# Values of the attention stream done for two steps at once, with small work in odd steps

## The chip, the cores and the metric

The kernel runs on one core of a Trainium2 chip. The core has a matrix engine (PE, TensorE), a vector engine (DVE), a scalar engine (ACT), GpSimd (POOL) and a queue engine (SP), which run side by side and meet at semaphores; 128 partitions of on-chip memory (SBUF); and PSUM, eight banks of 128 x 512 fp32[...]. The metric is the device time of one launch in microseconds; a run's result is the median of its repetitions.

## The reference

One transformer layer on x of shape (2, 2048, 256), all fp32: attention, a layer norm, then a feed-forward part with eight experts, and a last layer norm.

```python
qkv = x @ qkv_w + qkv_b                        # 16 heads of 16
q, k = rot(q), rot(k)                          # angle by head, not by position
scores = einsum('bhqd,bhkd->bhqk', q, k) / 4
out = einsum('bhqk,bhkd->bhqd', softmax(scores), v)
x = layernorm(x + out @ out_w + out_b)
n = layer_norm(x, g1, be1)
x1 = x + n + (n @ mix_w + mix_b)
n = layer_norm(x1, g2, be2)                    # 4096 tokens
topw, topi = top_k(softmax(n @ router_w), 2)   # 2 of 8 experts
y = silu(n @ w1[e] + b1[e]) @ w2[e] + b2[e]    # 256 -> 1024 -> 256
x = layernorm(x + x1 + sum over the two experts of topw * y)
```

Attention is the larger part: for each of 2 x 16 heads, 2048 x 2048 scores.

## The kernel before, in words

**Tiling of the attention.** A visit is one batch entry, one block of 512 queries and one group of four heads: 2 x 4 x 4 = 32 visits. A visit has 16 steps, one for each tile of 128 keys, so the stream has 512 steps (`NSTEP`). Queries and keys lie in two pair tiles (`qm`, `km`), two heads each, in 64 partitions per head: 16 head dimensions four times over, as high and low parts of the fp32 values[...].

**A step.** `scores` runs for both pairs: for each of four heads one matmul of keys by queries and one that subtracts the row's maximum, both on 64 rows of the array, two heads side by side. ACT takes the exponential of each 128 x 512 tile into SBUF (`ex`, L484-485, eight buffers). `values` multiplies the exponentials of a step by the values: four heads, each on 32 columns of the array at once; PE records eight matmuls for a call, two waves of four. The products of a visit's 16 steps add up in one PSUM bank (`av`), with a row of ones giving the softmax's sum. After the last step `attn_out` copies the bank to SBUF (`avs`), and `divide` turns it and divides by the sum.

**The maxima ahead.** The row maxima for a visit are computed 20 steps ahead (`AHEAD`) by `maxima`: each half step does two matmuls of 128 queries by 512 keys into two banks, and DVE reduces each bank to one column (`pm`, L434). A step has two halves, `max_step(t + AHEAD, 0)` and `max_step(t + AHEAD, 1)`. When a visit's maxima are done, `maxima_done` puts them in form on DVE and `rows_of` transposes them two steps later.

**Banks.** Four banks hold scores (`ps_sc`), one `av`, and three serve in rotation as `ps_mx`: the maxima take two per half, and every small item of PE takes its bank from the same three (`bank`).

**Small work.** All else in the stream is cut into items. `later(steps, fn, cost, urgent)` puts an item in one of two heaps by its due step; `work(budget)` takes due items until their costs use up the budget. Items of cost 2.0 are the projections to q and k (`prep_qk`), to v (`prep_v`), and the two products of a block's chain (`project`, `mix`, by way of `two_products`: eight matmuls, then on DVE an add, L568, and batch statistics, L571-572). `logits`, `bias` and `add_bias` cost 1.0, groups of four transposes 0.5 (`turned`, `prep_x`, `rows_of`, `divide`), the choice of experts 0.1 and 0.3 (`second`, `places`); loads and what runs on ACT, DVE or POOL alone cost nothing. The chain of a block of 512 tokens starts when its four visits are done, and is spread over the next 64 steps; that of the last block runs between the matmuls of the experts.

**The order.** The loop over t writes the order of PE, ACT, DVE and SP by hand (`manual_schedule`): scores of step t, first half of the maxima, small work, values of step t - 1, second half of the maxima. Each engine executes in that order; POOL is scheduled by the framework.

**Around it.** Ahead of the loop the weights are rotated (`wqk`, from `wr` and the table `cs`, with scratch tiles `t1`, `t2`), the first keys and queries are prepared, and the first 20 steps of maxima run. After it the tokens, sorted by expert into lists in DRAM, go through 46 tiles of experts (`load_tile`, `hidden`, `add_tile`), and the last layer norm.

Of the kernel before, what the change touches and what calls it, by code (L numbers as in the profile page):

```python
# [24 lines left out]
F32 = mybir.dt.float32  # L25
# [3 lines left out]
ALU = mybir.AluOpType  # L29
# [3 lines left out]
P = 128  # L33
B, S, D = 2, 2048, 256
H, HD = 16, 16
# [28 lines left out]
def seq_postln_kernel(  # L64
# [85 lines left out]
    bp = ctx.enter_context(tc.tile_pool(name="chain", bufs=1))  # L150
    ps_mx = ctx.enter_context(tc.tile_pool(name="ps_mx", bufs=3, space=PSUM))

    with ExitStack() as actx:

        ep = actx.enter_context(tc.tile_pool(name="early", bufs=1))
        ap_ = actx.enter_context(tc.tile_pool(name="attn", bufs=1))
# [4 lines left out]
        wqk = ep.tile([P, 2, 2, H, HD], F32, name="wqk")  # L161
# [23 lines left out]
        def load_x(b, tb):  # L185
            n = b * TPB + tb

            pool, tag, bufs = (ap_, f"km{tb % 2}", 3) if b == 0 else (ep, "x_in", 1)
            x_in[b, tb] = pool.tile([P, 4, D], F32, name=f"x_in_{n}", tag=tag, bufs=bufs)
            nc.sync.dma_start(out=x_in[b, tb], in_=xv[n])  # L190

        with tc.tile_pool(name="wraw", bufs=1) as wp:
            wr = bp.tile([P, 2, H, 3, HD], F32, name="wr", tag="zx", bufs=1)
            cs = wp.tile([P, 2, H, 8], F32, name="cs")
            load_x(0, 0)
            nc.scalar.dma_start(
                out=wr.rearrange("p c h t d -> p c (h t d)"),
# [59 lines left out]
            for c in range(2):  # L257
                for s in range(2):
                    u1, u2 = wr[:, c, :, s, 0:8], wr[:, c, :, s, 8:16]
                    for dst, a, b_, op in (  # L260
                        (wqk[:, c, s, :, 0:8], u1, u2, ALU.subtract),
                        (wqk[:, c, s, :, 8:16], u2, u1, ALU.add),
                    ):
                        t1 = wp.tile([P, H, 8], F32, name="t1", tag="t1", bufs=2)
                        t2 = wp.tile([P, H, 8], F32, name="t2", tag="t2", bufs=2)
                        nc.vector.tensor_mul(t1, a, cs[:, 0])
                        nc.vector.tensor_mul(t2, b_, cs[:, 1])
                        nc.vector.tensor_tensor(dst, t1, t2, op)
                nc.vector.tensor_copy(wv[:, c], wr[:, c, :, 2, :])
# [16 lines left out]
        now = [0]  # L286
# [6 lines left out]
            heappush(todo[0 if urgent else 1], (now[0] + steps, count[0], cost, fn))  # L293

        def work(budget):
            for heap in todo:
                while heap and heap[0][0] <= now[0] and budget > 0:
                    _, _, cost, fn = heappop(heap)
                    fn()
                    budget -= cost  # L300

        held: set = set()

# [10 lines left out]
        def bank(name, *shape):  # L314

            if leading[0]:
                return ps_sc.tile([P, *shape], F32, name=name, tag="sc")
            return ps_mx.tile([P, *shape], F32, name=name, tag="mx")
# [147 lines left out]
        def scores(w, kt, pair):  # L466
            sc = [ps_sc.tile([P, 512], F32, name="ps_sc", tag="sc") for _ in range(2)]
            for j in range(2):
                r = slice(64 * j, 64 * j + 64)
                nc.tensor.matmul(  # L470
                    sc[j],
                    lhsT=km[w][pair][r, kt * P : (kt + 1) * P],
                    rhs=qm[w][pair][r, :],
                    start=True,
                    stop=False,
                )
            for j in range(2):
                r = slice(64 * j, 64 * j + 64)
                nc.tensor.matmul(  # L479
                    sc[j], lhsT=sel[pair][r, :], rhs=mrow[w][r, :], start=False, stop=True  # L480
                )
            out = []
            for j in range(2):
                ex = ap_.tile([P, 512], F32, name="ex", tag="ex", bufs=8)  # L484
                nc.scalar.activation(ex, sc[j], AF.Exp, scale=0.25)  # L485
                out.append(ex)
            return out
# [4 lines left out]
        def values(w, kt, exs):  # L492
            b, _, g = visits[w]
            if kt == 0:
                av_of[w] = ps_av.tile([P, 512], F32, name=f"av_{w}", tag="av")
            av = av_of[w]
            for h in range(4):

                at = 17 * (4 * g + h)
                nc.tensor.matmul(  # L500
                    av[32 * h : 32 * h + 32, :],
                    lhsT=vt[b][:, kt, at : at + 32],
                    rhs=exs[h],
                    start=(kt == 0),
                    stop=(kt == 15),
                )
            if kt == 15:
                attn_out(w)

        def attn_out(w):  # L510

            b, qb, g = visits[w]
            av = av_of.pop(w)
            avs = bp.tile([P, 512], F32, name="avs", tag="avs", bufs=2)
            nc.scalar.copy(avs, av)
            if g == 0:
                otok[b, qb] = bp.tile([P, 4, D], F32, name=f"otok_{b}_{qb}", tag="otok", bufs=1)

            def divide():
                ps = bank("ps_o", 4, P)  # L520
                for i in range(4):
                    nc.tensor.transpose(ps[:, i, :], avs[:, i * P : (i + 1) * P], ident)  # L522
                psv = ps.rearrange("p i (h c) -> p i h c", c=32)
                rd = bp.tile([P, 4, 4], F32, name="rd", tag="rd", bufs=2)
                nc.vector.reciprocal(rd, psv[:, :, :, HD])
                nc.vector.tensor_tensor(
                    otok[b, qb][:, :, g * 64 : (g + 1) * 64].rearrange(
                        "p i (h d) -> p i h d", d=HD
                    ),
                    psv[:, :, :, 0:HD],  # L530
                    rd.unsqueeze(3).to_broadcast([P, 4, 4, HD]),
                    ALU.mult,
                )
                if g == G - 2:
                    residual(b, qb)
                if g == G - 1:
                    later(1, lambda: holding("chain", block, b, qb))

            later(1, divide, 0.5, urgent=True)
# [524 lines left out]
        with tc.manual_schedule(engines={ET.PE, ET.Activation, ET.DVE, ET.SP}):  # L1064
            for t in range(AHEAD):
                now[0] = t - AHEAD
                for half in range(2):
                    max_step(t, half)
                work(1.0)
            leading[0] = False  # L1070
            before = None
            for t in range(NSTEP):
                now[0] = t
                w, kt = divmod(t, 16)
                exs = scores(w, kt, 0) + scores(w, kt, 1)
                max_step(t + AHEAD, 0)
                work(1.0)
                if before is not None:
                    values(*before)
                max_step(t + AHEAD, 1)  # L1080
                before = (w, kt, exs)
            values(*before)
            now[0] = NSTEP

    wtp = ctx.enter_context(tc.tile_pool(name="weights", bufs=1))
# [111 lines left out]
    with tc.manual_schedule(engines={ET.PE, ET.Activation, ET.DVE, ET.SP}):  # L1197
# [3 lines left out]
        before = None  # L1201
        for t in range(NTILE):
# [8 lines left out]
            before = (t, xg, w2t, hT)  # L1211
# [119 lines left out]
```

## Time and profile before

| | us |
|---|---|
| median of 3 runs | 2401.39 (2400.65 to 2401.86) |
| the profiled execution | 2406.82 |
| its span, first to last instruction | 2405.1 |
| of it ahead of the stream's first score | 123.7 |
| the stream, 512 steps | 123.7 to 1793.3 |
| experts and last norm | 1793.3 to 2405.1 |
| busy PE / DVE / ACT / POOL | 2277.9 / 1534.9 / 1374.4 / 512.7 |
| busy in the stream (1669.6) PE / DVE / ACT | 1634.1 / 1351.4 / 1168.2 |

The times that follow come from one profiled execution. PEld is the loading of the stationary operand, which overlaps PE. A line of groups gives line, engine, operation, output<-inputs, shapes and count, then busy time and mean ns of one, then the idle time of the engine ahead of them with what ended it. The chain that ended last is followed back from the last instruction, at each step to what released it. PE's records are starts as measured and ends as modelled, so the text reckons with starts. The mean granted clock of TensorE is 0.972; it is 1.00 from about 200 to 1800 us.

### The profile page before, as it was taken

Reading aid. Unit: us, or ns where it says so; the run is one execution under the profiler, and the core shown is the slowest. Engines: PE = TensorE matmul, PEld = TensorE weight load, DVE = VectorE, ACT = ScalarE, POOL = GpSimd, SP = SyncE. Lnnn points to the kernel's source line nnn. Section 1 sums busy time; section 2 is a strip of 40 time slices with the busy share of each in tenths; the row PEclk is TensorE's granted clock in tenths of the full one; section 3 lists DMA queues with packets and bytes.
Section 4 is the critical chain, followed back from the end, with each engine's and each line's share of the span. In section 5 each row is a group of like instructions: output and inputs, shape, how many; then the busy total and the mean of one; then the engine's idle time right before and its main releaser. Section 6 shows DMA issues by size and latency. Waiting matters only on the chain.

```text
span 2405.1 us, 39739 instructions
## 1 busy us (share of the span) xinstructions
PE 2277.9 (95%) x14270; PEld 1363.8 (57%) x14270; DVE 1534.9 (64%) x3060; ACT 1374.4 (57%) x2722; POOL 512.7 (21%) x863
## 2 busy tenths in 40 slices
PE   5899999999999999999999999999998899999993
PEld 2444555545545555555555555555547788888883
DVE  2678778868877887888888888888825111111113
ACT  1167667757766776777777667777773222223333
POOL 6212221140123022011211202202122322222113
PEclk7799999999999999999999999999999899999997
DMA  7516541141124211111311211221045466567994
GB/s 217 153 42 182 144 115 54 54 132 53 53 72 123 87 55 58 58 45 54 115 45 54 71 45 53 89 71 53 1 138 168 142 193 180 176 182 225 291 292 151
DMA packets 175516, 269.69 MB, mean 112 GB/s; under 512 B 29776, under 2 KB 109656, under 8 KB 175320
## 3 DMA queue, kind: packets, MB, share of 16 engines
q1 hardware_dynamic: 142648, 213.26, 25.9%
q0 software_dynamic: 32256, 52.98, 10.1%
q8 instruction: 113, 1.85, 0.3%
q10 hardware_dynamic: 416, 0.92, 0.1%
q14 instruction: 83, 0.68, 0.1%
HBM read 204.29 MB, written 62.74 MB: 111 GB/s over the span
## 4 chain that ended last, share of the span: by engine, by line
PE 77%; DVE 16%; DMA 3%; ACT 2%; issue 1%; POOL 1%; another core or an unknown queue 0%; SPq 0%; ACTq 0%; DVEq 0%; POOLq 0%
PE av L500 19%; PE ps_mx L426 13%; DVE pm L434 12%; PE ps_h L1161 11%; PE ps_y L1176 10%; PE ps_sc L470 6%; PE ps_sc L479 6%; PE ps_qk L345 2%; DMA st<-full 2%; PE ps_v L371 1%; PE ps_p L561 1%; PE ps_mix L561 1%; PE ps_m L458 1%; PE ps_o L522 1%; PE ps_b L766 1%
## 5 line engine op out<-in xcount | busy, mean ns | idle before, releaser
L434 DVE TENSOR_REDUCE pm<-ps_mx 128x1 f32<-128x512 f32 x2048 | 1273.2, 682 | 218.3 <-PE ps_mx L426 209.3
L485 ACT ACTIVATE ex<-ps_sc 128x512 f32<-128x512 f32 x2048 | 1058.1, 603 | 453.7 <-PE ps_sc L479 433.7
L426 PE MATMUL ps_mx<-km,qm 64*128 64x512 f32 x2048 | 580.5, 474 | 36.4 <-DMA km<-st 15.3
L426 PEld LDWEIGHTS ps_mx<-km,qm 64*128 64x128 f32 x2048 | 297.7, 186 | 556.2 <-DVE pm L434 357.4
L500 PE MATMUL av<-ex,vt 128*32 128x512 f32 x4096 | 547.3, 606 | 0.0
L470 PE MATMUL ps_sc<-qm,km 64*128 64x512 f32 x2048 | 435.4, 396 | 0.4 <-ACT ex L485 0.3
L479 PE MATMUL ps_sc<-mrow,sel 64*128 64x512 f32 x2048 | 428.6, 392 | 0.0
L1168 ACT ACTIVATE hT<-ps_h,b 128x256 f32<-128x256 f32 (+1 forms) x368 | 156.3, 425 | 378.3 <-PE ps_h L1161 361.9
L1161 PE MATMUL ps_h<-xT,w 128*128 128x256 f32 (+1 forms) x1472 | 282.6, 342 | 17.2 <-issue 11.0
L1161 PEld LDWEIGHTS ps_h<-xT,w 128*128 128x128 f32 x1472 | 231.6, 193 | 62.4 <-ACT hT L1168 21.7
L1176 PE MATMUL ps_y<-w,hT 128*128 128x256 f32 x1136 | 253.7, 379 | 0.0
L479 PEld LDWEIGHTS ps_sc<-mrow,sel 64*128 64x128 f32 x2048 | 216.7, 185 | 40.5
L470 PEld LDWEIGHTS ps_sc<-qm,km 64*128 64x128 f32 x2048 | 214.8, 186 | 42.0 <-ACT ex L485 18.3
L1176 PEld LDWEIGHTS ps_y<-w,hT 128*128 128x128 f32 x1136 | 212.1, 190 | 27.5 <-issue 0.7
L1140 DVE TENSOR_SCALAR xT<-ps_x,cols_sb 128x256 f32<-128x256 f32 (+1 forms) x92 | 40.2, 478 | 271.4 <-PE ps_x L1136 271.4
L1187 POOL DMA_INDIRECT acc<-y,xg x71 | 110.1, 1551 | 390.8 <-DVE y L1186 307.0
L500 PEld LDWEIGHTS av<-ex,vt 128*32 128x32 f32 x4096 | 80.9, 108 | 133.7 <-issue 132.6
L1186 DVE TENSOR_SCALAR y<-ps_y,xg 128x256 f32<-128x256 f32 x71 | 34.2, 483 | 187.8 <-PE ps_y L1176 187.6
L132 POOL TENSOR_SCALAR op_mul<-mv 128x4 f32<-128x4 f32 x18 | 4.2, 233 | 492.7 <-DVE mv L572 491.7
L358 POOL TENSOR_TENSOR full<-full,hi 128x512 f32<-128x512 f32 x32 | 40.9, 1279 | 239.5 <-DVE hi L354 239.4
L345 PE MATMUL ps_qk<-xT,wqk 128*128 128x512 f32 x128 | 73.3, 700 | 4.8 <-ACT xT L336 1.5
L857 POOL DMA_INDIRECT x_list<-zx,at_i x64 | 64.1, 1002 | 16.5 <-issue 13.6
(198 smaller groups left out, 1160.4 us busy)
## 6 DMA issues: line engine op xcount, KB each, us to landing
w<-in_w SPq DMA_DIRECT2D x92, 1024.0 KB
km<-st SPq DMA_DIRECT2D x256, 256.0 KB
st<-hi POOLq DMA_DIRECT2D x64, 256.0 KB
st<-full POOLq DMA_DIRECT2D x64, 256.0 KB
qm<-st SPq DMA_DIRECT2D x64, 256.0 KB
xg<-x_list SPq DMA_DIRECT2D x25, 258.0 KB
x_in<-in_x SPq DMA_DIRECT2D x8, 512.0 KB
xr<-in_x SPq DMA_DIRECT2D x8, 512.0 KB
```

Of the source, the lines that this page charges most:

```text
L345: nc.tensor.matmul(ps, lhsT=wqk[:, c, s, 8 * hh : 8 * hh + 8, :].rearrange("p h d -> p (h d)"), rhs=xT[b, tb][:, c, :], start=(c == 0), st ...
L426: nc.tensor.matmul(ps[j], lhsT=qm[w][pair][r, qt * P : (qt + 1) * P], rhs=km[w][pair][r, kb * 512 : (kb + 1) * 512], start=True, stop=True,)
L434: nc.vector.tensor_reduce(pm[w][:, qt, 2 * pair + j, kb : kb + 1], ps[j], AX.X, ALU.max)
L470: nc.tensor.matmul(sc[j], lhsT=km[w][pair][r, kt * P : (kt + 1) * P], rhs=qm[w][pair][r, :], start=True, stop=False,)
L479: nc.tensor.matmul(sc[j], lhsT=sel[pair][r, :], rhs=mrow[w][r, :], start=False, stop=True)
L485: nc.scalar.activation(ex, sc[j], AF.Exp, scale=0.25)
L500: nc.tensor.matmul(av[32 * h : 32 * h + 32, :], lhsT=vt[b][:, kt, at : at + 32], rhs=exs[h], start=(kt == 0), stop=(kt == 15),)
L857: ins = nc.gpsimd.indirect_dma_start(out=x_list, out_offset=bass.IndirectOffsetOnAxis(ap=at_i[:, k, i : i + 1], axis=0), in_=zx[:, k, i, : ...
L1161: nc.tensor.matmul(ps, lhsT=w1t[:, c, k * P : (k + 1) * P], rhs=xT[:, c, :], start=(c == 0), stop=(c == 1),)
L1168: nc.scalar.activation(hT[:, k, :], ps, AF.Silu, bias=b1[:, k : k + 1])
L1176: nc.tensor.matmul(ps, lhsT=hT[:, k, s * P : (s + 1) * P], rhs=w2t[:, k, :], start=(k == 0), stop=(k == NFC - 1),)
L1187: nc.gpsimd.indirect_dma_start(out=acc, out_offset=bass.IndirectOffsetOnAxis(ap=xg[:, s, D : D + 1].bitcast(I32), axis=0), in_=y, in_offse ...
```

## The change

In an odd step due small work is done with the budget 1.0. If its costs come to 0.4 or more, no values are computed in that step, and the next even step computes those of both steps, one after the other, between the halves of its maxima. If they come to less, the odd step computes its values as before. In even steps only items of cost 0 are taken (`work(0)`); `work` now counts what it spent and returns it. The exponentials get twelve buffers instead of eight. To make room, `avs` has one buffer instead of two, and the rotation's table and scratch tiles move from a pool of their own to tiles that the blocks' chain uses later (`x2`, `fT`).

```diff
--- before.py
+++ after.py
@@ -191,7 +191,8 @@
 
         with tc.tile_pool(name="wraw", bufs=1) as wp:
             wr = bp.tile([P, 2, H, 3, HD], F32, name="wr", tag="zx", bufs=1)
-            cs = wp.tile([P, 2, H, 8], F32, name="cs")
+            cs = bp.tile([P, 2, H, 8], F32, name="cs", tag="x2", bufs=1)
+            rot = bp.tile([P, 4, 2, H, 8], F32, name="rot", tag="fT", bufs=1)
             load_x(0, 0)
             nc.scalar.dma_start(
                 out=wr.rearrange("p c h t d -> p c (h t d)"),
@@ -257,12 +258,13 @@
             for c in range(2):
                 for s in range(2):
                     u1, u2 = wr[:, c, :, s, 0:8], wr[:, c, :, s, 8:16]
-                    for dst, a, b_, op in (
-                        (wqk[:, c, s, :, 0:8], u1, u2, ALU.subtract),
-                        (wqk[:, c, s, :, 8:16], u2, u1, ALU.add),
+                    for k, (dst, a, b_, op) in enumerate(
+                        (
+                            (wqk[:, c, s, :, 0:8], u1, u2, ALU.subtract),
+                            (wqk[:, c, s, :, 8:16], u2, u1, ALU.add),
+                        )
                     ):
-                        t1 = wp.tile([P, H, 8], F32, name="t1", tag="t1", bufs=2)
-                        t2 = wp.tile([P, H, 8], F32, name="t2", tag="t2", bufs=2)
+                        t1, t2 = rot[:, 2 * (s % 2) + k, 0], rot[:, 2 * (s % 2) + k, 1]
                         nc.vector.tensor_mul(t1, a, cs[:, 0])
                         nc.vector.tensor_mul(t2, b_, cs[:, 1])
                         nc.vector.tensor_tensor(dst, t1, t2, op)
@@ -293,11 +295,20 @@
             heappush(todo[0 if urgent else 1], (now[0] + steps, count[0], cost, fn))
 
         def work(budget):
+
+            spent = 0.0
             for heap in todo:
-                while heap and heap[0][0] <= now[0] and budget > 0:
-                    _, _, cost, fn = heappop(heap)
-                    fn()
-                    budget -= cost
+                kept = []
+                while heap and heap[0][0] <= now[0] and (spent < budget or budget == 0):
+                    item = heappop(heap)
+                    if budget == 0 and item[2] > 0:
+                        kept.append(item)
+                        continue
+                    item[3]()
+                    spent += item[2]
+                for item in kept:
+                    heappush(heap, item)
+            return spent
 
         held: set = set()
 
@@ -481,7 +492,7 @@
                 )
             out = []
             for j in range(2):
-                ex = ap_.tile([P, 512], F32, name="ex", tag="ex", bufs=8)
+                ex = ap_.tile([P, 512], F32, name="ex", tag="ex", bufs=12)
                 nc.scalar.activation(ex, sc[j], AF.Exp, scale=0.25)
                 out.append(ex)
             return out
@@ -511,7 +522,7 @@
 
             b, qb, g = visits[w]
             av = av_of.pop(w)
-            avs = bp.tile([P, 512], F32, name="avs", tag="avs", bufs=2)
+            avs = bp.tile([P, 512], F32, name="avs", tag="avs", bufs=1)
             nc.scalar.copy(avs, av)
             if g == 0:
                 otok[b, qb] = bp.tile([P, 4, D], F32, name=f"otok_{b}_{qb}", tag="otok", bufs=1)
@@ -1068,18 +1079,21 @@
                     max_step(t, half)
                 work(1.0)
             leading[0] = False
-            before = None
+
+            waiting: list = []
             for t in range(NSTEP):
                 now[0] = t
                 w, kt = divmod(t, 16)
                 exs = scores(w, kt, 0) + scores(w, kt, 1)
                 max_step(t + AHEAD, 0)
-                work(1.0)
-                if before is not None:
-                    values(*before)
+                if t % 2 == 0 or work(1.0) < 0.4:
+                    work(0)
+                    while waiting:
+                        values(*waiting.pop(0))
                 max_step(t + AHEAD, 1)
-                before = (w, kt, exs)
-            values(*before)
+                waiting.append((w, kt, exs))
+            while waiting:
+                values(*waiting.pop(0))
             now[0] = NSTEP
 
     wtp = ctx.enter_context(tc.tile_pool(name="weights", bufs=1))
```

## The prediction

> **What bounds the kernel now.** I read the page's utilisation rows first, then the chain that ended last, then the groups of instructions, then the chain and the timeline inside single steps of the stream. From the page, its first part, the chain by line, and two groups:
>
> ```profile
> PE 2277.9 (95%) x14270; PEld 1363.8 (57%) x14270; DVE 1534.9 (64%) x3060; ACT 1374.4 (57%) x2722; POOL 512.7 (21%) x863
> ...
> PE av L500 19%; PE ps_mx L426 13%; DVE pm L434 12%; PE ps_h L1161 11%; PE ps_y L1176 10%; PE ps_sc L470 6%; PE ps_sc L479 6%; PE ps_qk L345 2%; DMA st<-full 2%; PE ps_v L371 1%; PE ps_p L561 1%; PE ps_mix L561 1%; PE ps_m L458 1%; PE ps_o L522 1%; PE ps_b L766 1%
> ...
> L434 DVE TENSOR_REDUCE pm<-ps_mx 128x1 f32<-128x512 f32 x2048 | 1273.2, 682 | 218.3 <-PE ps_mx L426 209.3
> ...
> L426 PEld LDWEIGHTS ps_mx<-km,qm 64*128 64x128 f32 x2048 | 297.7, 186 | 556.2 <-DVE pm L434 357.4
> ```
>
> PE looks like the bound, but the chain alternates between PE and the max reductions of DVE (L434, 12%), and the weight loads of the maxima were released by those reductions for 357.4 us. The two engines are tied by three PSUM banks (ps_mx). The stream takes 123.7 to 1793.3 us of the span, 512 steps, 3.27 us each. The chain in a step without small work:
>
> ```profile
> 966.42 0.23 PE ps_sc L470 x2
> 966.65 0.23 PE ps_sc L479 x2
> 966.88 0.23 PE ps_sc L470 x2
> 967.11 0.23 PE ps_sc L479 x2
> 967.34 0.35 PE ps_mx L426 x2
> 967.69 0.99 PE av L500 x8
> 968.69 0.43 PE ps_mx L426 x2
> ```
>
> So 0.92 us of scores (S), first maxima (M1), values (A), second maxima (M2), and 2.70 us in all. From the timeline, counted from the first score: M1 at 0.92, A at 1.36, M2 at 2.36, next S at 2.70. A is two waves, 0.45 us to the next wave and 0.54 to M2. DVE does four reductions in 2.48 us, one each 0.60 us: those of the last step's M2 begin at 0.20 and 0.80, those of this M1 at 1.40 and 2.00. DVE has 0.3 us to spare per step. A step with one group of four transposes takes 3.46.
>
> **Who waits for whom.** Each step takes four banks in rotation, a small item one more. With one small item between M1 and M2, M2's second matmul gets the bank of M1's second matmul, so it needs the reduction that began at 2.00. The delay from a reduction's slot to the matmul that needed its bank is read here (timeline of a step with the mix product and of the step after it):
>
> ```profile
> 1066.14 1.07 PE L500 MATMUL av<-ex,vt 128*32 128x512 f32 x8
> 1066.35 0.69 DVE L568 TENSOR_TENSOR x<-x,ps_mix 128x512 f32<-128x512 f32 x1 [0.99 <-PE ps_mix L561]
> 1067.07 0.43 DVE L571 BATCH_NORM_STATS2 st<-x 128x6 f32<-128x256 f32 x1
> 1067.14 0.50 PE L426 MATMUL ps_mx<-km,qm 64*128 64x512 f32 x2
> ...
> 1068.16 1.85 DVE L434 TENSOR_REDUCE pm<-ps_mx 128x1 f32<-128x512 f32 x3
> ...
> 1068.87 0.18 PEld L426 LDWEIGHTS ps_mx<-km,qm 64*128 64x128 f32 x1 [0.52 <-DVE pm L434]
> 1069.30 0.16 PEld L500 LDWEIGHTS av<-ex,vt 128*32 128x32 f32 x8 [0.25 <-issue]
> ```
>
> The reduction begins at 1068.16, its bank is used at 1068.87: 0.60 + about 0.12. It could begin so late only because the add, two statistics and two aggregates of the small item stand before it on DVE. Note that A (1066.14) ran while DVE did these.
>
> **What the change does.** Counting the items that the queue hands out in each step of the two programs: of 256 odd steps, 152 have work of cost 0.4 or more; there A is left out and the next even step does two. The other 104 pairs keep one A per step. Small PE items stand in 188 steps before and 159 after.
>
> *Saved: one switch of the array.* An item ahead of A means going from 128x128 tiles to 128x32 ones; after the change the item goes straight to the 64-row matmuls of M2. The last transpose of a group starts 0.21 before A, against a pitch of 0.11: the switch costs 0.10. Where the profile has an item directly before maxima (ps_v at 92.16, maxima at 94.08, 1.92 us), it takes what it takes before A (1.93), so M2 can follow when A did. [...]181 fewer switches (1212 to 1031) at 0.10 is -18 us. [...]
>
> *Lost: the cover of A.* All offsets count from the odd step's first score.
> - Short item emptied by ACT (rows_of, bias): item 1.54 to 2.12; M2's second matmul at 2.00+0.60+0.14 = 2.74, where A used to fill the time. Next S 2.75 (a late second matmul gives S at once, but M1 then comes 1.03 later: 3.78). Two A: 0.42 + 3 x 0.45 + 0.54 = 2.32, M2 at 6.11, next S 6.45. Before: 3.46 + 2.70 = 6.16. +0.3.
> - divide: its reciprocal and product (0.25 + 0.42 on DVE, from 2.60) come before M2's reductions, which begin at 3.30; the even M1's second matmul needs that bank, 4.04 and not 3.78. Pair 6.70 against 6.22. +0.5.
> - project, mix (eight matmuls, then add, statistics): M2's reduction begins at 5.43 as before, so the even M1's second matmul is at 6.15 as before. Before, one A had run by then and one was left; now two are left: 6.15 + 2.32 + 0.34 = 8.8 against 7.9. +0.9.
> - prep_qk: ACT's copy 3.57 to 4.26, DVE's mask (hi, 0.43) to about 4.76, only then M2's reduction, to 5.36; even M1 at 5.50, end 8.16 against 7.49. +0.67.
> - Two transpose groups now in one odd step (turned, z, zx, prep_x): the third bank waits for ACT's copy, M2 at 3.41, pair 7.13, the pair freed of the other group 5.40; 12.53 against 12.32. +0.2 (turned, whose other group sat beside divide: 0).
> - logits, prep_v: long on PE (to 3.42), nothing on DVE: both banks are free, only the switch counts. -0.1.
>
> Work on DVE of cost nil in the even step (norms, lists, the maxima's end) moves into the DVE pause of some 1 us that two A make, and is taken off: after the second project the pair with rows_of loses nothing more (15.3 for both pairs against 15.0), after the second mix 0.65 and not 0.9.
>
> *Sum of a settled block* (steps 256 to 319, 989.0 to 1193.5): divide 4 x 0.5; rows_of 0.3; turned, z, zx 0.4; first project 0.9; second with rows_of 0.3; first mix 0.9; second 0.65; logits -0.1; second and places -0.15 (merged with rows_of); bias and both add_bias 0.2. Together 5.4 us. Four such blocks 21.6. Steps 0 to 63: fourteen prep_qk, rows_of, divide, 9.8. Steps 64 to 191: two blocks with prep as well; there bias, add_bias and places, which had steps of 3.5 to 3.9 of their own, come to share steps, 3.6 each. The last block has no maxima from step 492 on, 3.7. Sum 9.8 + 7.2 + 21.6 + 3.7 = **42 us**.
>
> *Parts at nothing.* Twelve ex tiles: a tile is rewritten three steps on and its values are read by then; the cover gone, ACT would wait up to 2.3 us per pair. One avs: read one step after it is written, next written 16 steps on. cs and rot: the same 24 products, in tiles whose next writers come 66 steps later. The store of acc on SP's queue moves behind two loads of qm, and behind the first expert weights at the end; it then holds nobody. The block's row scatters on POOL and prep_qk's stores move 1 to 9 steps; the last scatters and the first tile list move one step, so the first expert tile is asked for some 2.3 us later, 25 us before its use; without that cover 2.3 us. After the stream the order is the same.
>
> *Unknown.* Two A in a row: 0.45 between waves (taken, the row inside one A), or 0.54 as at its end: up to 152 x 0.09 = +14. From below the pure PE account, -18.
>
> The profiled execution took 2406.8 us, of which the span is 2405.1. 2406.8 + 42 = 2449; the median of the runs is 5.4 lower, so 2401.4 + 42 = **2443 us**.
>
> **Rivals.**
> 1. PE alone decides. The place is M2's second matmul in an odd step: were its bank free by 2.14, a short pair would take 6.05 instead of 6.16, and 152 x -0.11 = -17: 2384. It decides where the item ends later than 2.74 and leaves DVE nothing, as with logits and prep_v. For it: PE 95% busy. Against: the other 137 pairs miss one condition or the other.
> 2. Half the loss, 2422: DVE's pause in the even step absorbs the backlog of product items too. Against: the matmul that waits stands ahead of both A on PE, so nothing can be absorbed before it.
> 3. More, 2463: two A don't run on (+14), and late exponentials push the scores in double steps. Against: ACT is idle 0.63 us per quiet step and four score banks.
> 4. Nothing happens: pairing only where small work is due. 104 pairs are untouched, but 152 are not.
>
> **Numbers.** Chances: likeliest 0.71, its own range 2432 to 2454; rival 1 0.07; rival 2 0.10; rival 3 0.10; no change 0.02. The range for 8 in 10 is 2415 to 2466. A measurement here tells about 0.2% (4.8 us) from no change: faster 0.07, same 0.03, slower 0.90.
>
> **What would show it.** Pairs of 5.40 untouched; in double steps M1's second matmul waiting for a reduction of pm, with DVE then idle about 1 us before M2; odd steps with transposes 2.75 long, the even ones 3.7; project and mix pairs near 8.8; the reductions' idle time released by ps_mx up by more than 100 us. Wrong if M2's second matmul in odd steps follows the first at once, or if the even M1 in product pairs does not wait.

## The result and the profile after

| | before | after |
|---|---|---|
| median of the runs, us | 2401.02 (2400.01 to 2401.86, 4 runs) | 2455.70 (2453.23 to 2458.01, 4 runs) |
| ratio, 95% interval | | 1.0228 (1.0210 to 1.0245) |
| the profiled execution, us | 2406.82 | 2458.01 |
| ahead of the stream / the stream / behind it, us | 123.7 / 1669.6 / 611.8 | 122.1 / 1726.7 / 607.5 |

The change costs 54.7 us, 2.3%. The forecast was 42. In the profiled executions the stream is 57.1 us longer; the parts around it give back 5.9.

The page of the kernel after, its first part, the chain by line and four groups (line numbers are 11 higher than before, L445 is the reduction that was L434):

```profile
PE 2277.0 (93%) x14270; PEld 1376.0 (56%) x14270; DVE 1536.5 (63%) x3060; ACT 1372.4 (56%) x2722; POOL 510.2 (21%) x863
...
PE 72%; DVE 15%; ACT 5%; issue 4%; DMA 2%; POOL 1%; another core or an unknown queue 0%; ACTq 0%; SPq 0%; DVEq 0%; POOLq 0%
...
L445 DVE TENSOR_REDUCE pm<-ps_mx 128x1 f32<-128x512 f32 x2048 | 1277.0, 683 | 276.4 <-PE ps_mx L437 259.9
L496 ACT ACTIVATE ex<-ps_sc 128x512 f32<-128x512 f32 x2048 | 1057.9, 603 | 517.5 <-PE ps_sc L490 508.9
L437 PE MATMUL ps_mx<-km,qm 64*128 64x512 f32 x2048 | 609.7, 472 | 92.1 <-DVE pm L445 38.9
L437 PEld LDWEIGHTS ps_mx<-km,qm 64*128 64x128 f32 x2048 | 301.9, 186 | 556.3 <-DVE pm L445 380.2
```

No engine has more to do: PE 2277.0 against 2277.9 us, DVE 1536.5 against 1534.9, ACT 1372.4 against 1374.4. All of the loss is waiting. The idle time of the reductions that ended with a maximum from PE went from 209.3 to 259.9 us, and the weight loads of the maxima waited 380.2 us for reductions, against 357.4. The exponentials wait longer too, 508.9 us for their scores against 433.7: they follow the stream, they don't set it. ACT's share of the chain grew all the same, from 2% to 5%; its copies of small items come up below. The two lines of before for this:

```profile
PE 77%; DVE 16%; DMA 3%; ACT 2%; issue 1%; POOL 1%; another core or an unknown queue 0%; SPq 0%; ACTq 0%; DVEq 0%; POOLq 0%
...
L485 ACT ACTIVATE ex<-ps_sc 128x512 f32<-128x512 f32 x2048 | 1058.1, 603 | 453.7 <-PE ps_sc L479 433.7
```

The chain that ended last, across the first project of a block and the even step after it (start, length, what):

```profile
1035.51 1.29 DVE pm L445 x2
1036.80 0.04 issue
1036.84 1.14 PE ps_p L572 x5
1037.98 0.95 issue
1038.93 0.70 DVE xr L579
1039.63 0.02 issue
1039.65 0.44 DVE st L582
1040.09 0.02 issue
1040.11 0.18 DVE mv L583
1040.30 0.32 DVE st L582
1040.62 0.02 issue
1040.64 0.18 DVE mv L583
1040.82 0.58 DVE pm L445
1041.41 0.04 issue
1041.45 0.50 PE ps_mx L437
1041.95 1.85 PE av L511 x16
```

This is the central step of the prediction. The odd step starts at 1035.3 and M2 stands straight behind the product (1038.76 in the timeline). The even step's first M1 matmul is at 1040.03. Its second is at 1041.45: it needs the bank of M2, whose reduction waits behind the add, two statistics and two aggregates of the product. Only then come both A, sixteen matmuls in 1.85 us. In the kernel before, one A stood in front of that wait.

### The profile page after: what moved, and what is told of

It reads as the page before. It is cut to its first block, busy times and chain, and to the rows that moved or that the text cites. A ratio compares the mean times of both kernels' runs of the same rounds, so it can differ in the third digit from the quotient of the medians.

```text
span 2456.3 us, 39740 instructions
## 1 busy us (share of the span) xinstructions
PE 2277.0 (93%) x14270; PEld 1376.0 (56%) x14270; DVE 1536.5 (63%) x3060; ACT 1372.4 (56%) x2722; POOL 510.2 (21%) x863
## 3 DMA queue, kind: packets, MB, share of 16 engines
q8 instruction: 113, 1.85, 0.3%
## 4 chain that ended last, share of the span: by engine, by line
PE 72%; DVE 15%; ACT 5%; issue 4%; DMA 2%; POOL 1%; another core or an unknown queue 0%; ACTq 0%; SPq 0%; DVEq 0%; POOLq 0%
PE av L511 19%; PE ps_mx L437 13%; PE ps_h L1175 10%; DVE pm L445 10%; PE ps_y L1190 10%; PE ps_sc L481 6%; PE ps_sc L490 6%; ACT ex L496 3%; PE ps_v L382 1%; PE ps_mix L572 1%; PE ps_p L572 1%; DMA st<-full 1%; PE ps_qk L356 1%; DVE st L582 1%; ACT full L363 1%
## 5 line engine op out<-in xcount | busy, mean ns | idle before, releaser
L445 DVE TENSOR_REDUCE pm<-ps_mx 128x1 f32<-128x512 f32 x2048 | 1277.0, 683 | 276.4 <-PE ps_mx L437 259.9
L496 ACT ACTIVATE ex<-ps_sc 128x512 f32<-128x512 f32 x2048 | 1057.9, 603 | 517.5 <-PE ps_sc L490 508.9
L437 PE MATMUL ps_mx<-km,qm 64*128 64x512 f32 x2048 | 609.7, 472 | 92.1 <-DVE pm L445 38.9
L437 PEld LDWEIGHTS ps_mx<-km,qm 64*128 64x128 f32 x2048 | 301.9, 186 | 556.3 <-DVE pm L445 380.2
L511 PE MATMUL av<-ex,vt 128*32 128x512 f32 x4096 | 518.2, 605 | 0.0
L481 PE MATMUL ps_sc<-qm,km 64*128 64x512 f32 x2048 | 449.4, 399 | 0.1
L490 PE MATMUL ps_sc<-mrow,sel 64*128 64x512 f32 x2048 | 439.9, 393 | 0.0
L490 PEld LDWEIGHTS ps_sc<-mrow,sel 64*128 64x128 f32 x2048 | 228.6, 185 | 41.0
L481 PEld LDWEIGHTS ps_sc<-qm,km 64*128 64x128 f32 x2048 | 223.9, 186 | 37.5 <-ACT ex L496 16.2
L511 PEld LDWEIGHTS av<-ex,vt 128*32 128x32 f32 x4096 | 97.0, 109 | 186.5 <-issue 184.6
```

Source lines behind the costliest of these rows:

```text
L437: nc.tensor.matmul(ps[j], lhsT=qm[w][pair][r, qt * P : (qt + 1) * P], rhs=km[w][pair][r, kb * 512 : (kb + 1) * 512], start=True, stop=True,)
L445: nc.vector.tensor_reduce(pm[w][:, qt, 2 * pair + j, kb : kb + 1], ps[j], AX.X, ALU.max)
L481: nc.tensor.matmul(sc[j], lhsT=km[w][pair][r, kt * P : (kt + 1) * P], rhs=qm[w][pair][r, :], start=True, stop=False,)
L490: nc.tensor.matmul(sc[j], lhsT=sel[pair][r, :], rhs=mrow[w][r, :], start=False, stop=True)
L511: nc.tensor.matmul(av[32 * h : 32 * h + 32, :], lhsT=vt[b][:, kt, at : at + 32], rhs=exs[h], start=(kt == 0), stop=(kt == 15),)
```

## The experiments

All variants ran on other chips of the same kind, beside the kernel before, whose median there was 2384.7 to 2386.4 us; the difference to 2401 lies behind the stream (some 595 us there, 608 to 612 on the first chip). So ratios are compared, and lengths inside the stream. The table gives both; the stream is that of the profiled execution, from the first score of step 0 to the first score of step 511.

| kernel | median us | ratio (95%) | stream us |
|---|---|---|---|
| before | 2385.89 | 1 | 1669.6 (first chip) |
| after, again | 2438.62 | 1.0228 (1.0211 to 1.0245) | 1720.2 |
| small work in odd steps, values never paired | 2372.32 | 0.9950 (0.9932 to 0.9967) | 1654.9 |
| before, small work in odd steps | 2376.24 | 0.9955 (0.9940 to 0.9970) | 1657.6 |
| paired beside short work only | 2415.29 | 1.0132 (1.0113 to 1.0152) | 1695.2 |
| paired beside long work only | 2396.97 | 1.0057 (1.0037 to 1.0076) | 1678.1 |
| paired always | 2487.47 | 1.0441 (1.0424 to 1.0459) | 1770.5 |
| after, first values early behind products | 2420.92 | 1.0152 (1.0133 to 1.0171) | 1702.9 |
| after, statistics later | 2427.52 | 1.0178 (1.0160 to 1.0197) | 1710.1 |
| before, statistics later | 2411.65 | 1.0112 (1.0093 to 1.0130) | 1692.3 |
| after, banks in strict turn | 2426.15 | 1.0173 (1.0159 to 1.0187) | 1707.2 |
| before, banks in strict turn | 2384.96 | 0.9995 (0.9986 to 1.0003) | 1669.4 |

In the expectations, theory A is the prediction's: values between a small item and M2 cover the time in which banks come free, and pairing takes the cover away. The other theories are named where they stand. The table below is the evidence that most verdicts use: the mean length of an odd step and the even step after it, in us, by what small work the odd step has in the kernel after. It leaves out the last 20 steps, which have no maxima, pairs with two kinds of work, and a few other kinds.

| work (pairs) | before | after | never paired | short only | long only | always |
|---|---|---|---|---|---|---|
| none (92) | 5.64 | 5.48 | 5.50 | 5.53 | 5.48 | 6.01 |
| divide (23) | 6.49 | 6.57 | 6.22 | 6.57 | 6.22 | 6.57 |
| project (14) | 7.93 | 8.73 | 7.93 | 7.93 | 8.73 | 8.73 |
| mix (7) | 7.96 | 8.82 | 7.96 | 7.96 | 8.82 | 8.81 |
| prep_qk (12) | 7.63 | 8.02 | 7.62 | 7.51 | 8.02 | 8.02 |
| prep_v (6) | 7.86 | 7.35 | 7.50 | 7.70 | 7.35 | 7.36 |
| rows_of (12) | 6.77 | 7.13 | 6.77 | 7.39 | 6.35 | 7.09 |
| two groups of turned (7) | 6.38 | 7.31 | 6.75 | 7.31 | 6.75 | 7.30 |
| bias (4) | 7.26 | 7.03 | 6.19 | 7.03 | 6.19 | 7.03 |
| logits (7) | 7.71 | 8.24 | 8.08 | 8.10 | 7.68 | 8.05 |

### Everything but the pairing

```diff
-                if t % 2 == 0 or work(1.0) < 0.4:
-                    work(0)
-                    while waiting:
-                        values(*waiting.pop(0))
+                work(0 if t % 2 == 0 else 1.0)
+                while waiting:
+                    values(*waiting.pop(0))
```

> All of the change but the pairing: small work in odd steps only, twelve tiles of exponentials, one avs, and the values of one step in every step. Theory A (the loss is the cover that the values gave to bank waits, lost where two values stand together): 2395 to 2403, as two groups of transposes that meet in one step with values between save some 0.15 us per meeting. Theory B (small work held back to odd steps, or the smaller buffers, cost the time): 2440 to 2456.

Measured: 0.9950, 12 us faster than before. The stream is 14.7 us shorter than before, and 65.3 shorter than in the repeat of the kernel after (1720.2). So the change has two parts of opposite sign: small work in odd steps gains half a per cent, and pairing the values costs 2.8% on top. From the page of this variant:

```profile
PE 2265.2 (95%) x14270; PEld 1360.0 (57%) x14270; DVE 1531.7 (64%) x3060; ACT 1374.1 (58%) x2722; POOL 512.3 (22%) x863
...
L445 DVE TENSOR_REDUCE pm<-ps_mx 128x1 f32<-128x512 f32 x2048 | 1270.6, 682 | 209.4 <-PE ps_mx L437 209.1
...
L437 PEld LDWEIGHTS ps_mx<-km,qm 64*128 64x128 f32 x2048 | 293.5, 186 | 547.5 <-DVE pm L445 325.7
```

The maxima wait 325.7 us for reductions where the kernel before waits 357.4 and the kernel after 380.2.

### Only small work in odd steps, in the kernel before

```diff
-                work(1.0)
+                work(0 if t % 2 == 0 else 1.0)
```

with the new `work`, and without the other edits (eight `ex`, two `avs`, the old `cs`).

> The kernel before with small work of cost above nil in odd steps only, and nothing else of the change (eight tiles of exponentials, two avs, the old rotation tiles). If the gain of the run without pairing comes from the order of the small work: 0.995. If it comes from the buffers or the moved tiles: 1.000.

Measured: 0.9955, the same as the variant above within its interval. So the gain is that of the order, and twelve exponentials, one `avs` and the moved scratch tiles are worth nothing that shows. Where it comes from is in the pairs. Two groups of transposes in one odd step and a free pair take 6.75 + 5.40 us against 2 x 6.16 for z; one change from 128x128 to 128x32 tiles less, 0.10 us as the prediction read it, may be part of these 0.17 us, but no run separates it. The pair of rows_of and second falls from 8.53 to 6.66 while that of places rises from 5.40 to 6.19, so 1.08 us are gained, four times. This is a bank wait again: in the kernel before, second's seven small operations on DVE stand ahead of the reductions of the rows_of step, and M1's second matmul there waits 1.08 to 1.10 us for one of them (at 931.2, 1136.0, 1340.6 and 1545.9 us). With both items in one odd step, second's operations stand behind that step's reductions, and this wait is gone.

### Pairing beside short work only, and beside long work only

```diff
-                if t % 2 == 0 or work(1.0) < 0.4:
+                if t % 2 == 0 or not 0.4 <= work(1.0) < 2.0:
```

> The changed kernel, but values are paired only after odd steps whose small work cost at least 0.4 and less than 2.0 (transposes, logits, bias, add_bias); after projections and products they stay one per step. Theory A: the pairs with project, mix and prep_qk no longer lose 0.80, 0.86 and 0.53 us, and prep_v no longer gains 0.15: 28 x 0.83 + 22 x 0.53 - 8 x 0.15 = 34 us less than the changed kernel, 2422. Theory C (every pair costs the same, 55/152 = 0.36 us, for what two values do together): 58 pairs fewer, 2435.

```diff
-                if t % 2 == 0 or work(1.0) < 0.4:
+                if t % 2 == 0 or work(1.0) < 2.0:
```

> The complement: values are paired only after odd steps whose small work cost 2.0 or more. Theory A: the kernel without pairing plus 34 us, 2429 to 2437. Theory C: 58 pairs at 0.36, 2416 to 2424.

Measured: 1.0132 and 1.0057, that is 2433 and 2415 us on the scale where before is 2401. By the totals alone one price for every pair (2435, and 2416 to 2424) does better than theory A (2422, and 2429 to 2437). The pairs decide against it. The price of pairing differs by kind, in the order that A worked out: +0.80 for project, +0.86 for mix, +0.40 for prep_qk, -0.15 for prep_v, +0.35 for divide, each measured against never pairing. A single price per pair doesn't allow both +0.86 and -0.15. A missed the totals elsewhere. In the short half the 28 products fell by 23.1 us, as A had it (23.2), but prep_qk fell by 8 us and not by 11.7, and the pairs of rows_of and of no work rose by 8.5 together. In the long half the base was lower than A expected, 2389 instead of 2395 to 2403, and the rows_of pairs fell by 5.1. Counted from never pairing, the two halves cost 40.3 and 23.2 us of stream, 63.5 together, against 65.3 for both: they add up.

Long only also shows the give-back that the prediction names: where the second project stands before it, the rows_of pair falls from 7.03 to 6.31 when the product is paired. Together the two pairs take 15.01 us, paired or not. In both kernels DVE works without a pause from the product's add to the reductions of the rows_of step, at the same times to 0.01 us: there DVE sets the length, wherever A stands.

### Pairing in every even step

```diff
-                if t % 2 == 0 or work(1.0) < 0.4:
+                if t % 2:
+                    work(1.0)
+                else:
```

> Values are paired in every even step, also where the odd step has no small work. Theory A: in an odd step with nothing between the halves of the maxima, the second half waits for the first reduction (2.14), and the even first half for the next ones (3.34), so that a quiet pair takes 6.0 instead of 5.4: some 90 pairs, +50 us on the changed kernel, 2506. Theory D (PE alone[...]): 2420.

Measured: 1.0441, 2507 on the scale of 2401. Theory A asked for 2506, rival 1 (PE alone decides, so fewer switches are a gain) for 2420, an estimate. A pair with no work at all goes from 5.40 to 5.95. By the prediction's offsets, without A between them M2's first matmul can go at 1.54, its second only at 2.14. DVE idles while both A run: behind the two A at 1041.95 in the kernel after its next reduction, at 1044.26, has 1.07 us of idle time ahead of it. The page:

```profile
PE 2295.2 (92%) x14270; PEld 1376.0 (55%) x14270; DVE 1527.6 (62%) x3060; ACT 1374.2 (55%) x2722; POOL 510.1 (21%) x863
...
L445 DVE TENSOR_REDUCE pm<-ps_mx 128x1 f32<-128x512 f32 x2048 | 1269.9, 681 | 320.7 <-PE ps_mx L437 311.7
...
L437 PEld LDWEIGHTS ps_mx<-km,qm 64*128 64x128 f32 x2048 | 316.4, 186 | 548.2 <-DVE pm L445 404.4
```

DVE's busy time is 9 us less than after, and its idle time released by maxima 311.7 us against 259.9. Rival 1 is refuted: with the fewest switches of all, this is the slowest kernel. A second A right behind the first costs 0.86 us where one alone takes 0.99, so a visit less to the values saves 0.13 us by these rows.

### The first of the two values put back in front of the wait

In even steps behind project and mix, one A goes ahead of M1 and the other stays behind it; the number of A and of DVE's instructions is that of the kernel after, but for one visit more to the 128x32 tiles in those steps. `products` is set by `two_products`.

```diff
                 exs = scores(w, kt, 0) + scores(w, kt, 1)
+                if t % 2 == 0 and products[0] and len(waiting) == 2:
+                    values(*waiting.pop(0))
+                products[0] = False
                 max_step(t + AHEAD, 0)
```

> The changed kernel, but in even steps that follow a project or mix the first of the two values stands ahead of the first maxima, so that it covers their wait; one more change of tiling mode per such pair. Theory A: first values from 1.34 to 2.33 of the even step, the maxima's second matmul at 2.35 as before, then one value only: 0.8 us less in 28 pairs, 22 us less than the changed kernel, ratio about 1.0135. Theory C: nothing gained[...].

Measured: 1.0152, for which theory A gave 1.0135, and the other theory, by which nothing is gained, 1.023. The 28 pairs with a product fell by 0.79 to 0.86 us each, to 7.94 (project) and 7.96 (mix), which is their length in the kernel before, and to 8.71 where rows_of stands beside mix (8.70 before). The same place in the chain:

```profile
1025.91 0.43 PE ps_mx L437 x2
1026.34 0.23 PE ps_sc L481 x2
1026.58 0.23 PE ps_sc L490 x2
1026.81 0.23 PE ps_sc L481 x2
1027.04 0.23 PE ps_sc L490 x2
1027.28 0.99 PE av L511 x8
1028.27 0.75 PE ps_mx L437 x2
1029.02 1.00 PE av L511 x8
```

DVE doesn't appear any more. Its reductions lie where they lay (1.64, 2.21, 2.81 and 3.41 us from the step's first score in both kernels), and M1's second matmul starts 2.35 from it in both. Only what PE does meanwhile differs. That is the cover, shown by itself. The total gains less than the pairs, because the rows_of pair behind the second project goes from 7.09 to 7.53, and a few quiet pairs grow too.

### The statistics of a product done a step later

```diff
-            for i in range(2 * k, 2 * k + 2):
-                st = bp.tile([P, 6], F32, name="st", tag="st", bufs=3)
-                nc.vector.bn_stats(st, sum_[:, i, :])
-                nc.vector.bn_aggr(mv[:, i, :], st)
+            def stats():
+                for i in range(2 * k, 2 * k + 2):
+                    ...
+            later(1, stats)
```

In the kernel after:

> The changed kernel with one edit: the batch statistics of project and mix (two statistics, two aggregates, 1.1 us on DVE) are an item of their own in the next step, and so stand behind the reductions of the odd step's second maxima, not ahead of them. Theory A (the loss is a bank wait that the values no longer cover): those reductions start after the add, 1.1 us earlier, the even step's first maxima wait 1.1 us less, and the statistics fall into the pause of DVE while two values run: 28 x 1.1 = 31 us less than the changed kernel, ratio to before about 1.010. Theory C (two values cost what they cost on PE, whatever DVE does): no change, 1.023.

and in the kernel before:

> The same edit in the kernel before. Theory A: there the values of the odd step already covered the statistics, and one value leaves DVE no pause in the next step, so the late statistics delay that step's second reductions: no gain, a ratio of 1.002 to 1.008. Theory C, and anyone who takes the statistics for a plain cost of the path: the same gain as in the changed kernel, 0.987 to 0.995.

Measured: 1.0178 and 1.0112. In the kernel after, the pairs with a product fell as A said, by 1.18 us each (8.73 to 7.55), 33 us in all. But two thirds came back elsewhere. The work of the statistics met the maxima's end and the norms in the rows_of step behind the second project, which went from 7.09 to 8.0. Four of the seven pairs of that kind grew further, to 9.6 and 11.0. The profile's stretches of one of them show why (PE, PEld, DVE, ACT and POOL busy, then the granted clock of PE, DMA share, GB/s):

```profile
388.20:392.20 4.00, 4.00 (x34) 1.90 (x32) 3.86 (x11) 2.07 (x4) 0.00 (x0) 1.00 0.00 0
392.20:395.40 3.20, 2.08 (x13) 1.04 (x9) 3.06 (x11) 2.24 (x5) 1.77 (x9) 1.00 0.01 3
395.40:398.80 3.40, 3.19 (x16) 1.92 (x19) 2.03 (x4) 2.03 (x5) 1.23 (x6) 0.51 0.00 0
398.80:402.20 3.40, 3.40 (x16) 0.51 (x16) 0.92 (x2) 0.45 (x1) 0.00 (x0) 0.50 0.00 0
402.20:406.00 3.80, 3.80 (x32) 2.25 (x30) 2.96 (x5) 2.55 (x5) 0.00 (x0) 0.99 0.48 145
```

PE was idle for a third of one stretch, and then ran at half clock for 6.8 us. In the kernel before the same edit makes it slower, as A said and against the theory that counts only the work moved. But its size is 1.1%, not the 0.2 to 0.8% that A gave: the product pairs fall by 0.4, the quiet pair behind a first product goes from 5.40 to 6.15, the rows_of pairs behind a second one from 7.03 to 8.27, and three of the seven to 9.7 at half clock.

### The banks in strict turn

The one row of the prediction's table that was far off is that of short items which ACT empties (7.03 to 7.20 where 6.45 was forecast). The suspicion: the pool gives M2's second matmul the item's own bank. This variant gives the three banks out in strict turn.

```diff
-    ps_mx = ctx.enter_context(tc.tile_pool(name="ps_mx", bufs=3, space=PSUM))
+    ps_mx = ctx.enter_context(tc.tile_pool(name="ps_mx", bufs=1, space=PSUM))
+    turn = [0]
+    def next_bank():
+        turn[0] += 1
+        return f"mx{turn[0] % 3}"
...
-            return ps_mx.tile([P, *shape], F32, name=name, tag="mx")
+            return ps_mx.tile([P, *shape], F32, name=name, tag=next_bank())
```

> The kernel after, with the three PSUM banks of maxima and small items taken in strict turn instead of by the pool's choice. Bank theory (the pairs of rows_of and bias are longer than forecast because M2's second matmul got the item's own bank and waits for ACT's copy behind four exponentials): that matmul now starts at 2.74 and not at 3.25 to 3.43, rows_of pairs fall from 7.1-7.2 to 6.4-6.6, bias from 7.03 to 6.5, undisturbed logits pairs from 7.66 to 7.36; together some 8 + 2 + 2 = 12 us of the stream's 1726.7, ratio to the kernel before about 1.018. Rival (the length comes from the two values in a row and the late exponentials of the even step, whatever bank is used): those pairs stay within 0.1 us of 7.03 to 7.20, ratio 1.021 to 1.0245. Pairs of divide, project, mix and prep_qk stay as they are in both.

The same in the kernel before, as a control:

> The kernel before, with the same strict turn of the three banks. Bank theory: with values between the item and M2 the item's bank is free again (copy ends at 3.35, M2 starts at 3.12), so little changes: rows_of pairs stay at 6.40 and 7.03, ratio 0.997 to 1.002. Rival (strict turn alone is faster, whatever is done with the values): ratio at or below 0.995.

and the kernel after unchanged beside both:

> The kernel after unchanged, beside the two others on their chip. Ratio 1.021 to 1.0245 again if the chip doesn't matter. Pairs of add_bias, 7.2 in the profiled execution of the first chip and 6.67 to 6.74 in all variants with the same order: 6.7 here if that was one execution's, 7.2 if it is the program's. Granted clock: between one and five stretches of some 3.4 us at half clock in the stream, all at or just after logits.

Measured: 1.0173 (1.0159 to 1.0187) for the strict turn, 1.0228 (1.0211 to 1.0245) for the kernel after on the same chip, 0.9995 for the control. bias pairs fell from 7.03 to 6.51, rows_of from 7.14 to 6.69 (0.1 above the 6.4 to 6.6 expected), undisturbed logits from 7.66 to 7.31; divide, project, mix and prep_qk stayed within 0.01. A bias step in the timeline of the kernel after:

```profile
1190.44 0.60 PE L768 MATMUL ps_c<-ident,comb 128*8 128x128 f32 x4 [0.20 <-issue]
...
1190.97 0.49 PE L437 MATMUL ps_mx<-km,qm 64*128 64x512 f32 x1
1191.46 0.56 ACT L769 COPY cT<-ps_c 8x512 f32<-8x512 f32 x1
...
1192.07 0.50 PE L437 MATMUL ps_mx<-km,qm 64*128 64x512 f32 x1 [0.60 <-ACT ex L496]
```

and the same step with the banks in strict turn (line numbers 6 higher):

```profile
1176.09 0.60 PE L774 MATMUL ps_c<-ident,comb 128*8 128x128 f32 x4 [0.19 <-DVE pm L451]
...
1176.61 1.07 PE L443 MATMUL ps_mx<-km,qm 64*128 64x512 f32 x2
1177.11 0.56 ACT L775 COPY cT<-ps_c 8x512 f32<-8x512 f32 x1
1177.19 0.18 PEld L443 LDWEIGHTS ps_mx<-km,qm 64*128 64x128 f32 x1 [0.40 <-DVE pm L451]
```

In the first, the second M2 matmul starts 1.63 us behind the transposes, 0.05 after the end of ACT's copy (1191.46 + 0.56). In the second its weights load at 1177.19, 1.10 behind them, while the copy still runs, and what it waited for is a reduction: 2.74 from the step's first score, the number of the prediction. The first's brackets name an exponential on ACT rather than the copy behind it; the start times tell which it was.

## Why the prediction was right, and where its size failed

**What bounds the stream.** Right. PE and the reductions are tied by three banks. Pairing always cuts the switches to the fewest and is slowest of all; putting one A back in front of the wait takes the price of the products off.

**Project and mix.** Right: 8.8 forecast, 8.73 and 8.82 measured, with M1's second matmul in the even step at the time forecast (6.15 from the odd step's start, measured 3.81 + 2.35). One variant moved one A per pair, and that price went. One of their sums was not met: behind the second project the pair with rows_of was to lose nothing more, 15.3 us for both pairs, and 15.80 was measured. With the banks in strict turn it is 15.36, so this belongs to the step that failed.

**divide, prep_qk, prep_v.** Right within 0.15 us: 6.70 forecast and 6.57 measured; 8.16 and 8.02; -0.1 and -0.15 against never pairing. M2's second matmul behind divide is at 2.74, the forecast's number.

**Two transpose groups.** Right within 0.2: 12.53 for both pairs forecast; 7.31 + 5.40 measured.

**Two A in a row.** The value taken, 0.45 between waves, was the right end of its range: 0.45, 0.42, 0.42 and 0.53 measured. The dearer end, +14 us, is out.

**Parts at nothing.** Right: the odd-only order with and without them is 0.9950 and 0.9955.

**The step that failed.** "With one small item between M1 and M2, M2's second matmul gets the bank of M1's second matmul." That holds for divide, whose bank DVE empties. For rows_of and bias, which ACT empties, the program gives it the item's own bank, and so it waits for ACT's copy, which stands behind four exponentials: 3.25 and 3.43 instead of 2.74. In logits the first M2 matmul waits in the same way (ACT's copy 3.53 to 3.71, M2 at 3.77 and not 3.42), so the -0.1 became +0.2. The price of this assumption is measured: 1.0228 minus 1.0173 is 0.0055, 13 us of 2401, and the gap between 54.7 and 42 is 12.7. With the banks as the prediction took them the kernel has the ratio of the forecast, 1.0173 against 2443 / 2401.4 = 1.0173. That the two agree to the last digit is luck: the stream in strict turn is 37.6 us longer than before. By parts of the stream the forecast was 9.8 (steps 0 to 63), 7.2 (64 to 191), 21.6 (the four blocks) and 3.7 (the last); in strict turn it is 5.1, 6.9, 22.0 and 3.6, with some 2 us of doubt in each, for stretches at a lower clock differ from run to run (see the end). So the sum holds but for the first part, where prep_qk costs 0.28 to 0.55 us a pair and not 0.67; the terms given there, fourteen prep_qk, one rows_of and one divide, make 10.2 anyway, not 9.8.

The trace of before held the number. In a step with oT's transposes ACT's copy runs from 2.64 to 3.35 and M2's second matmul follows at 3.41, while M2's first is at 3.12. The step behind it, which starts at 998.65, shows the same wait:

```profile
1001.36 0.71 ACT L548 ACTIVATE oT<-ps_oT,rows_sb 128x512 f32<-128x512 f32 x1
...
1001.77 0.85 PE L426 MATMUL ps_mx<-km,qm 64*128 64x512 f32 x2
1002.12 0.18 PEld L426 LDWEIGHTS ps_mx<-km,qm 64*128 64x128 f32 x1 [0.17 <-ACT oT L548]
```

There the lateness cost little, for A had filled the time until 3.12. The prediction read the delay in the third bank of two groups (M2 at 3.41) but not in steps with one group.

**What the sum hid.** The blocks were summed as one change. Never pairing shows two: -14.7 us of stream for the order, about +65 for the pairing. The net was near the forecast, and in part by luck, since two terms of opposite sign were never told apart. The first was not written down by itself, and it is the one worth keeping.

**The signs to look for.** Quiet pairs of 5.40 and project pairs of 8.8 came as said. DVE's idle time released by maxima rose by 51 us, not by over 100; of the chain that ended last ACT now has 5% and had 2%, waits that the prediction had put on DVE. Odd steps with one group of transposes are 3.26 to 3.43 long where ACT empties them and 2.74 for divide; 2.75 was said of all.

**The change of tiling mode.** For the change spoke the 0.10 us that the prediction read for a switch: the last transpose of a group starts 0.20 us before A, against a pitch of 0.11. In the kernel after it starts 0.20 to 0.21 before M2 where M2 has its bank, so going straight to M2 has the same price. A gain shows where nothing else waits: prep_v pairs gain 0.15 by pairing (7.35 against 7.50). The rest of the stream was lengthened by waits for banks to be emptied: the weight loads of the maxima waited 380.2 us for reductions, against 325.7 with values never paired.

**Still open.** In the profiled execution on the first chip four add_bias pairs took 7.2 us and two more 7.3 and 9.5, where the repeat has 6.65 to 6.73 for all; DVE's and ACT's first instructions start late there without a wait that the profile shows. It is 5.5 us of that execution alone. The 9.5 in part has a known cause: from 802.9 to 806.4 us, inside that pair, the granted clock was 0.50. Why the pool chooses the item's bank stays open; taking a wait away without its cause was not tried, for it would be a race.

## What to carry to other kernels

Before work is taken out of an in-order queue to save its switching, look at what became free while it ran: here each visit to the values gave DVE and ACT the time to empty the banks that the next matmul needs, and a queue with 95% busy records still lost 2.8% by losing it. For each matmul behind the removed work, find the bank that it gets and which engine empties that bank; the bank of the item in front may be handed out again at once. Of a change with two parts measure each alone: small work in odd steps with values in every step runs at 0.9950 of before (0.9932 to 0.9967), which beats both kernels.

## What the runs showed of the hardware

PE's clock falls to half inside the stream. In the kernel before the granted clock is 0.50 from 917.2 to 920.6 us, so that its stream is not at 1.00 throughout, as the page's slices had it. In the kernel after, past the stream's first 9 us, it is 0.50 in four stretches of 3.4 us, from 499.2, 724.4, 802.9 and 946.3 on. Of the other eleven profiles, ten have stretches of 4 us at 0.50 to 0.72 between 200 and 572, 800 and 1168, or 1400 and 1764 us; with pairing beside long work only all of these are at 1.00. The stretches around a logits step of the kernel after, columns as above:

```profile
937.00:941.20 4.20, 3.93 (x32) 1.81 (x33) 2.67 (x4) 3.05 (x6) 0.00 (x0) 1.00 0.02 4
941.20:945.20 4.00, 3.63 (x30) 3.03 (x28) 2.48 (x4) 2.25 (x5) 0.00 (x0) 1.00 0.00 0
945.20:949.20 4.00, 4.00 (x24) 1.55 (x26) 2.54 (x4) 2.07 (x4) 0.00 (x0) 0.64 0.00 0
949.20:953.20 4.00, 4.00 (x32) 1.77 (x26) 2.58 (x5) 2.05 (x4) 0.00 (x0) 0.94 0.00 0
```

In finer stretches the granted clock is 0.50 from 946.3 to 949.7, 3.4 us, and the pair takes 9.28 us where its undisturbed fellows take 7.66. PE's records show it busy for 3.63 of the 4.00 us ahead, in a step of sixteen small matmuls with waits around them; what sets the half clock off was not tested. It fell so at one of seven logits pairs of before and at three of seven after; between the bounds named it fell twice in the repeat (936 to 944 and 1148 to 1156 us) and once with the strict turn (1564 to 1572). The page's slices, over 60 us wide, round it away. In the kernels with late statistics it also fell where PE waited for DVE, and there it took part of the expected gain: in the kernel after PE is busy for 2.08 of 3.20 us, and the clock is 0.51 and 0.50 in the 6.8 us behind them; in the kernel before it is busy for 2.38 of the 4.00 us from 1040 on, with a clock of 0.79 there and 0.78 in the next 4.00.

A bank is used 0.04 to 0.05 us after the engine that emptied it is done, by the rows above: 1041.45 behind a reduction that ends at 1041.41, 1002.12 behind a copy of ACT that ends at 1002.07, 1192.07 behind one that ends at 1192.02. Two A in a row take 1.85 us of the chain where one takes 0.99: a second A behind the first costs 0.86.
